# A decoder layer on one core: one joined ones product in each attention

## The chip, the core and the metric

The kernel runs on one core of a Trainium2 chip. Its time is the device time of one execution in microseconds (us); the figure given is the median of several executions. The engines of the core have these names in the profile: PE is TensorE's matmul unit and PEld its weight load, DVE is VectorE, ACT is ScalarE, POOL is GpSimd, and SP is the engine whose queue issues most DMA transfers. Each engine works through its own queue in order; semaphores tie the queues together.

## The reference, cut to what matters

Four inputs of 512 rows and 512 features pass through one decoder layer: a causal self-attention with 16 heads of 32, a causal cross-attention whose keys and values are both the context, and a feed-forward part. All data are float32. The part that the change touches is the softmax of both attentions:

```python
scores = jnp.einsum('bhqd,bhkd->bhqk', q, k) * SCALE
scores = jnp.where(causal, scores, -jnp.inf)
probs = jax.nn.softmax(scores, axis=-1)
ctx = jnp.einsum('bhqk,bhkd->bhqd', probs, v)
```

The cross-attention masks with -10000 in place of minus infinity, so that rows whose visible scores are all very low give weight to masked keys as well. The kernel computes these "masked weights" apart and adds them to numerator and denominator.

## The kernel before

**Layout.** The exponentials are held transposed: keys on the 128 partitions, queries along the free axis. The 16 heads are handled in 4 groups `g` of 4 heads, the 512 keys in 4 blocks `j` of 128. Block `j` of the keys is seen only by the queries from `j*128` on, so a block has 512, 384, 256 or 128 columns. `pts` are two tiles for a unit, each with two of the four heads.

**Units.** An attention (`attend`, L923) walks through ten units, written out by hand at L926 to L929. In this text they are called u0 to u9: (group, block) = (0,0); (0,3)(0,1); (0,2)(1,2); (1,0); (1,3)(1,1); (2,0); (2,3)(2,1); (2,2)(3,2); (3,0); (3,3)(3,1). For each unit `scores` (L385) lets TensorE multiply keys and queries and add the row maxima (L397, L408), ScalarE take the exponential (L431) and POOL zero the masked half of the diagonal blocks (L439). Two units later `values` (L451) lets TensorE use the exponentials. The loop issues the scores of unit n and then the values of unit n-2; the last two units' values come after the loop. All four compute engines run in exactly the order in which the code issues (`BY_HAND`), so what stands earlier in this text stands earlier in the queue.

**Numerator and denominator.** In `shares` (L458) a PSUM pair `pv` of a group has the numerator in half 0 (`u = 0`, exponentials times values) and, for some groups, the denominator in half 1 (`u = 1`, exponentials times a matrix of ones), both at L470. For the groups in `self.added` the denominator is made otherwise: VectorE adds the blocks' exponentials into one tile `sum` (`add_up`, L518), and a single ones product over it (`summed`, L524) gives the denominator. `self.added` is groups 0, 1, 2 in the self-attention and 0, 2 in the cross-attention. The other groups (3; and 1, 3) have one ones product for every block.

**What follows a denominator.** In the self-attention `inverse` (L545 to L548) transposes it, takes the reciprocal and transposes back, on VectorE; POOL scales group 0 to 2 (L540) and VectorE multiplies the last group (L509). The denominator of group 2 is made in a PSUM pair `ls` in unit u8 (L495 to L497). In the cross-attention `divide` (L558, L559) adds the masked weights first. After the self-attention the output projection (L695) follows on TensorE in four quarters, with transposes of the context and of the next input between them (`tp_c`, `tp_a`, L251).

**Masked weights.** `masked` (L373 on ScalarE) and `weigh` (L379 to L381) prepare them. In `attend` VectorE's `weigh` is called at n = 4, 6 or 9 if one is waiting (L956). In three of the four inputs group 2's is made at n = 3; for input 3 at n = 5, with the transposes `mt_c_both` (L353).

**Memory.** PSUM has four pairs in rotation (`ps`): two for a unit's scores, the rest for `pv`, `ls`, `mb` and the transposes. `pt` has six buffers. Tag `xin` has two buffers of 512 columns, into which SP loads the next input for its layer norm (L576).

Of the kernel before, what the change touches and what calls it, by code (L numbers as in the profile page):

```python
# [9 lines left out]
F32 = mybir.dt.float32  # L10
BF16 = mybir.dt.bfloat16
AF = mybir.ActivationFunctionType
ALU = mybir.AluOpType
# [5 lines left out]
P = 128  # L19
# [7 lines left out]
def decoder_layer(  # L27
# [21 lines left out]
    nc = tc.nc  # L49
    B, S, D = x.shape  # L50
    NH = 16
    HD = D // NH
    NT = S // P
    NC = D // P
    HG = P // HD
# [5 lines left out]
    work = ctx.enter_context(tc.tile_pool(name="work", bufs=2))  # L61
# [3 lines left out]
    def pair(name):  # L65

        return ps.tile([P, 2, S], F32, tag="ps", name=name)
# [61 lines left out]
    ones = const.tile([P, HD], F32, name="ones")  # L129
# [8 lines left out]
    zero = const.tile([P, 1], F32, name="zero")  # L138
# [123 lines left out]
    class Attention:  # L262
        def __init__(self, q_t, k_t, v, cross, name):
# [2 lines left out]
            self.more, self.sums, self.rden, self.e = {}, {}, {}, None  # L266
            self.added = (0, 2) if cross else range(NC - 1)

        def maxima(self, pieces):

            at, N = [], 0
            for g, i in pieces:
                at.append(N)
                N += (i + 1) * P
                if g not in self.nm:
                    self.nm[g] = small.tile(
                        [P, NT, HG], F32, tag="nm", name=f"nm_{self.name}_{g}"
                    )  # L280
            name = f"{self.name}_{pieces[0][0]}_{pieces[0][1]}"
            scs = [pair(f"sm_{name}_{n}") for n in range(2)]
            for (g, i), c in zip(pieces, at):
                for r in range(HG):
                    h = slice(r * HD, (r + 1) * HD)
                    nc.tensor.matmul(  # L286
                        scs[r // 2][:, r % 2, c : c + (i + 1) * P],
                        lhsT=self.q_t[h, g, i * P : (i + 1) * P],
                        rhs=self.k_t[h, g, : (i + 1) * P],
                        start=(c == 0),  # L290
                        stop=True,
                        skip_group_check=(c > 0),
                    )
            made = []
            for n in range(2):
                s = work.tile([P, 2, S], F32, tag="pt", name=f"s_{name}_{n}", bufs=6)
                nc.scalar.copy(s, scs[n])  # L297

                if len(pieces) == 1:
                    diagonal = s[:, :, S - P :].unsqueeze(2)  # L300
                elif pieces[0][1] == pieces[1][1]:
                    diagonal = s.rearrange("p u (k q) -> p u k q", k=2)[:, :, :, P:]
                else:
                    diagonal = s[:, :, S - 2 * P :].rearrange("p u (k q) -> p u k q", k=2)
                nc.gpsimd.affine_select(  # L305
                    out=diagonal,
                    in_=diagonal,
                    compare_op=ALU.is_ge,
                    fill=NEG,
                    base=0,  # L310
                    pattern=[[0, 2], [0, len(pieces)], [-1, P]],
                    channel_multiplier=1,
                )
                made.append(s)

            def largest(n, g, i, c):
                nc.vector.tensor_reduce(  # L317
                    self.nm[g][:, i, 2 * n : 2 * n + 2],
                    made[n][:, :, c : c + (i + 1) * P],
                    axis=AX.X,  # L320
                    op=ALU.max,
                    negate=True,
                )

            jobs = [
                (lambda n=n, g=g, i=i, c=c: largest(n, g, i, c))
                for n in range(2)
                for (g, i), c in zip(pieces, at)
            ]
            if pieces == [(pieces[0][0], NT - 1)]:  # L330
                jobs.append(lambda: self.split(pieces[0][0]))
            return jobs
# [125 lines left out]
        def shares(self, g, blocks):  # L458

            js = {j for j, *_ in blocks}  # L460
            first = js == {0} if g % 2 == 0 else js == {2}
            last = js == {2} if g % 2 == 0 else 1 in js
            if first:
                self.pv[g] = pair(f"pv_{self.name}_{g}")
            pv = self.pv[g]
            for u in range(1 if g in self.added else 2):
                for n, (j, c, pts) in enumerate(blocks):
                    for r in range(HG):
                        h = g * HG + r
                        nc.tensor.matmul(  # L470
                            pv[r * HD : (r + 1) * HD, u, j * P :],
                            lhsT=ones if u else self.v[:, j, h * HD : (h + 1) * HD],
                            rhs=pts[r // 2][:, r % 2, c : c + S - j * P],
                            start=first,
                            stop=last and n == len(blocks) - 1,
                            skip_group_check=True,
                        )
            if self.cross:


                if (first if g == 1 else js == {0}) and g - 1 in self.added:
                    self.summed(g - 1, self.pv[g - 1])
                    self.divide(g - 1)
                elif js == {0} and g > 0:
                    self.scale(g - 1)
                if 1 in js and g == NC - 1:
                    self.scale(g - 1)
                if last and g not in self.added:
                    self.divide(g)
                    if g == NC - 1:  # L490
                        self.scale(g)
                return
            if first and g == 0:
                self.out = act.tile([P, NC, S], F32, tag="o_t", name=f"oT_{self.name}")
            if (first if g in self.added else js == {0}) and g - 1 in self.added:  # L495
                self.sum_in = pv if g in self.added else pair(f"ls_{self.name}")
                self.summed(g - 1, self.sum_in)  # L497
            if js == {0} and g - 2 in self.added:
                self.scale(g - 2)
            if 1 in js and g - 1 in self.added and g not in self.added:  # L500
                self.spread(g - 1, self.sum_in)
                self.scale(g - 1)
            if last and g in self.added:
                nc.scalar.copy(self.out[:, g, :], pv[:, 0, :])
                if g > 0:
                    self.spread(g - 1, pv)
            elif last:
                num, den = pv[:, 0, :], pv[:, 1, :]
                nc.vector.tensor_tensor(  # L509
                    self.out[:, g, :], num, self.inverse(g, den), ALU.mult  # L510
                )

        def add_up(self, made):
            for g, j, c, pts in made:
# [408 lines left out]
    def attend(a, late):  # L923


        units = []  # L926
        for g in range(0, NC, 2):
            units += [[(g, 0)], [(g, 3), (g, 1)], [(g, 2), (g + 1, 2)]]
            units += [[(g + 1, 0)], [(g + 1, 3), (g + 1, 1)]]  # L929
        waiting, held, todo = [], [], []  # L930

        def values():
            made = waiting.pop(0)
            a.values(made)

            if len(made) > 1 and made[0][1] == 2:
                held.append(made[1:])
            elif waiting and waiting[0][0][1] > 0:
                if made[0][1] == 0 and held:
                    a.add_up(held.pop())  # L940
                a.add_up(waiting[0] if waiting[0][0][1] == 3 else waiting[0][:1])

        for n, pieces in enumerate(units):
            waiting.append(a.scores(pieces))
            if n in late:
                two = a.cross and late[n] == NC - 1
                both = pair(f"mt_{a.name}_both") if two else None
                copies = a.rows(late[n], both)

                more = [a.masked_sums(2, both)] if two else []  # L950
                for copy in copies:
                    copy(nc.scalar.copy)
                todo.extend(a.masked(*each) for each in more)
            if a.cross and n == 7:
                todo.append(a.masked(*a.masked_sums(3)))
            if n in (4, 6, 9) and todo:  # L956
                todo.pop(0)()
            if n in (3, 4) and put_off:
                put_off.pop(0)()
            if len(waiting) > 2:  # L960
                values()
        while waiting:
            values()

    with tc.manual_schedule(engines=BY_HAND):
# [11 lines left out]
        for b in range(B):  # L977
# [5 lines left out]
            late = with_maxima(between_self, sa, skip, norms)  # L983
# [13 lines left out]
            late = with_maxima(steps[3:], ca)  # L997
# [79 lines left out]
```

## Time and profile before

| what | us |
|---|---|
| median of 3 runs (806.68 to 806.87) | 806.86 |
| the profiled run's own time | 806.75 |
| its span, first to last instruction | 805.0 |
| DVE L518, adding exponentials, self-attention, 72 adds | 59.8 |
| POOL L439, masks of the exponentials, cross / self, 64 / 56 | 53.5 / 48.1 |
| PE L470, ones products of the cross-attention, 64 records each of 512, 384, 256, 128 columns | 8.3, 6.6, 4.9, 3.2 |
| PE L470, ones products of the self-attention, 32 records each of the same | 4.2, 3.3, 2.5, 1.6 |

A float32 product leaves two records, so 64 records of one shape are 32 products: 4 heads, 2 groups, 4 inputs. The four products of a group go to different quarters of the array's columns and run side by side, so the duration of one (592 ns for 512 columns) is much longer than its share of the time. A row of the timeline has the start and the duration in us, then the engine, the line, the operation, the tile written and the tiles read, the shape and how many; in brackets stands how long the engine was idle just before, and what it waited for. Neighbouring instructions of one kind are merged into one row.

### The profile page before, as it was taken

What the parts mean: (1) busy time and instruction counts of PE and PEld (TensorE: products, weight loads), DVE (VectorE), ACT (ScalarE), POOL (GpSimd) and SP (SyncE); (2) the same over time, 40 slices, a digit from 0 to 9 for tenths busy, and PEclk for the clock granted to TensorE, in tenths of its full rate; (3) what the DMA queues carried; (4) which work ended last, traced back from release to release, by engine and by line L of the source; (5) the groups of instructions that cost most, each with busy time, mean ns of one, the idle gap of its engine ahead of it and who ended that gap; (6) DMA issues with size and microseconds to landing.
All of it is one profiled execution on the core that took longest, in us unless ns stands there. A gap on an engine that the chain in (4) does not pass through costs nothing.

```text
span 805.0 us, 13960 instructions
## 1 busy us (share of the span) xinstructions
PE 796.0 (99%) x5612; PEld 380.4 (47%) x5616; DVE 561.4 (70%) x957; ACT 395.6 (49%) x448; POOL 335.8 (42%) x523
## 2 busy tenths in 40 slices
PE   8999999999999999999999999999999999999998
PEld 7444454444444454444544455444444444444544
DVE  2478855879679854587867786587959766988512
ACT  2457516871446615567055742687156833674110
POOL 4334612564234732256333482256423652475100
PEclk9999999999999999999999999999999999999999
DMA  9600000001000000021100000000102000000101
GB/s 336 239 28 28 1 1 1 2 2 53 1 27 27 2 1 0 2 74 33 53 14 14 1 2 1 0 1 2 54 26 80 2 2 0 1 2 2 52 1 52
DMA packets 13681, 24.51 MB, mean 30 GB/s; under 512 B 1968, under 2 KB 2224, under 8 KB 13616
## 3 DMA queue, kind: packets, MB, share of 16 engines
q1 hardware_dynamic: 13184, 22.96, 8.4%
q8 instruction: 44, 0.72, 0.4%
q10 hardware_dynamic: 432, 0.66, 0.2%
q14 instruction: 21, 0.17, 0.1%
HBM read 19.42 MB, written 4.19 MB: 29 GB/s over the span
## 4 chain that ended last, share of the span: by engine, by line
PE 92%; ACT 3%; DVE 3%; issue 1%; DMA 0%
PE pm_qk L235 13%; PE pm_d L223 7%; PE pm_u L235 7%; PE pm_o L695 7%; PE pv_c L470 7%; PE pm_e L223 7%; PE pm_v L223 6%; PE sm_c L286 6%; PE pv_s L470 5%; PE sm_s L286 5%; PE sc_c L397 5%; PE sc_s L397 4%; PE sc_s L408 1%; ACT sum_s L431 1%; DVE nm_s L317 1%; PE sc_c L408 1%
## 5 line engine op out<-in xcount | busy, mean ns | idle before, releaser
L317 DVE TENSOR_REDUCE nm_s<-s_s 128x2 f32<-128x1024 f32 (+3 forms) x128 | 96.9, 810 | 35.2 <-POOL s_s L305 35.2
L317 DVE TENSOR_REDUCE nm_c<-s_c 128x2 f32<-128x1024 f32 (+3 forms) x128 | 95.8, 810 | 31.0 <-POOL s_c L305 31.0
L297 ACT COPY s_s<-sm_s 128x1024 f32<-128x1024 f32 x80 | 77.1, 1015 | 70.7 <-PE sm_s L286 36.4
L297 ACT COPY s_c<-sm_c 128x1024 f32<-128x1024 f32 x80 | 77.1, 1016 | 35.9 <-PE sm_c L286 16.2
L305 POOL TENSOR_SCALAR_AFFINE_SELECT s_c<-s_c 128x512 f32<-128x512 f32 (+1 forms) x80 | 43.9, 550 | 100.4 <-ACT s_c L297 100.4
L305 POOL TENSOR_SCALAR_AFFINE_SELECT s_s<-s_s 128x512 f32<-128x512 f32 (+1 forms) x80 | 43.9, 551 | 96.9 <-ACT s_s L297 96.9
L518 DVE TENSOR_TENSOR sum_s<-sum_s,pt_s 128x256 f32<-128x256 f32 (+2 forms) x72 | 59.8, 896 | 16.7 <-PE pv_s L470 16.7
L431 ACT ACTIVATE pt_c<-sc_c 128x1024 f32<-128x1024 f32 x64 | 61.7, 1031 | 17.7 <-PE sc_c L408 13.8
L439 POOL TENSOR_SCALAR_AFFINE_SELECT pt_c<-pt_c 128x512 f32<-128x512 f32 (+1 forms) x64 | 53.5, 845 | 22.4 <-ACT pt_c L431 22.1
L223 PE MATMUL pm_d<-wdown_sb,hT 128*128 128x512 f32 x128 | 61.5, 610 | 0.0
L431 ACT ACTIVATE pt_s<-sc_s 128x1024 f32<-128x1024 f32 x56 | 53.9, 1029 | 12.6 <-PE sc_s L408 7.0
L235 PE MATMUL pm_u<-fT,wup_sb 128*128 128x512 f32 x128 | 59.3, 604 | 0.0
L223 PE MATMUL pm_v<-wv_sb,xnT 128*128 128x512 f32 x128 | 58.8, 600 | 0.0
L695 PE MATMUL pm_o<-wo_sb,oT_s 128*128 128x512 f32 x128 | 57.8, 596 | 0.0
L235 PE MATMUL pm_qk<-xnT,wk_sb 128*128 128x512 f32 x120 | 57.3, 607 | 0.0
L397 PE MATMUL sc_c<-cqT,ckT 32*128 32x384 f32 (+3 forms) x512 | 56.0, 464 | 0.9 <-ACT sum_c L431 0.9
L235 PE MATMUL pm_qk<-xnT,wq_sb 128*128 128x512 f32 x120 | 56.7, 604 | 0.0
L223 PE MATMUL pm_e<-wexp_sb,fT 128*128 128x512 f32 x120 | 56.3, 604 | 0.0
L397 PE MATMUL sc_s<-qT,kT 32*128 32x128 f32 (+3 forms) x512 | 54.4, 462 | 1.2 <-ACT sum_s L431 0.9
L439 POOL TENSOR_SCALAR_AFFINE_SELECT pt_s<-pt_s 128x512 f32<-128x512 f32 (+1 forms) x56 | 48.1, 868 | 17.6 <-ACT pt_s L431 17.0
L286 PE MATMUL sm_c<-ckT,cqT 32*128 32x512 f32 (+3 forms) x512 | 47.5, 460 | 0.0
L286 PE MATMUL sm_s<-kT,qT 32*128 32x512 f32 (+3 forms) x512 | 47.0, 461 | 0.0
(167 smaller groups left out, 1267.7 us busy)
## 6 DMA issues: line engine op xcount, KB each, us to landing
cv<-in_ctx_dram SPq DMA_DIRECT2D x16, 256.0 KB, 3.6
out_dram<-x SPq DMA_DIRECT2D x15, 256.0 KB, 2.1
x<-in_x_dram SPq DMA_DIRECT2D x14, 256.0 KB, 4.0
xin<-in_x_dram SPq DMA_DIRECT2D x12, 256.0 KB, 2.7
wq_sb<-in_wq_dram SPq DMA_DIRECT2D x2, 512.0 KB, 6.3
wk_sb<-in_wk_dram SPq DMA_DIRECT2D x2, 512.0 KB, 7.9
wv_sb<-in_wv_dram SPq DMA_DIRECT2D x1, 1024.0 KB, 8.3
wo_sb<-in_wo_dram SPq DMA_DIRECT2D x1, 1024.0 KB, 10.1
```

What stands on the lines that cost most here:

```text
L223: nc.tensor.matmul(pm, lhsT=lhs_t[:, c, t * P : (t + 1) * P], rhs=w[:, c, :], start=(c == 0), stop=(c == NC - 1),)
L235: nc.tensor.matmul(pm, lhsT=w[:, c, f * P : (f + 1) * P], rhs=rhs_t[:, c, :], start=(c == 0), stop=(c == NC - 1),)
L286: nc.tensor.matmul(scs[r // 2][:, r % 2, c : c + (i + 1) * P], lhsT=self.q_t[h, g, i * P : (i + 1) * P], rhs=self.k_t[h, g, : (i + 1) * P] ...
L297: nc.scalar.copy(s, scs[n])
L305: nc.gpsimd.affine_select(out=diagonal, in_=diagonal, compare_op=ALU.is_ge, fill=NEG, base=0, pattern=[[0, 2], [0, len(pieces)], [-1, P]], ...
L317: nc.vector.tensor_reduce(self.nm[g][:, i, 2 * n : 2 * n + 2], made[n][:, :, c : c + (i + 1) * P], axis=AX.X, op=ALU.max, negate=True,)
L397: nc.tensor.matmul(scs[r // 2][:, r % 2, c : c + S - j * P], lhsT=self.k_t[h, g, j * P : (j + 1) * P], rhs=self.q_t[h, g, j * P :], start= ...
L431: nc.scalar.activation(pt, scs[n], AF.Exp)
L439: nc.gpsimd.affine_select(out=diagonal, in_=diagonal, compare_op=ALU.is_ge, fill=0.0, base=0, pattern=[[0, 2], [0, len(pieces)], [1, P]], ...
L470: nc.tensor.matmul(pv[r * HD : (r + 1) * HD, u, j * P :], lhsT=ones if u else self.v[:, j, h * HD : (h + 1) * HD], rhs=pts[r // 2][:, r % ...
L518: nc.vector.tensor_tensor(to, to, pts[n][:, :, c : c + S - j * P], ALU.add)
L695: nc.tensor.matmul(pms[t // 2][:, t % 2, :], lhsT=a.out[:, c, t * P : (t + 1) * P], rhs=wo_sb[:, c, :], start=(c == 0), stop=(c == NC - 1),)
```

## The change

In each attention one group that has a ones product for every block is picked, `self.joined`: group 1 in the cross-attention and group 3 in the self-attention. Its block 2 (256 columns, queries 256 to 511) gets no ones product of its own. VectorE adds the exponentials of block 2 to the second half of those of block 0 (`join`) into two new tiles `jn` of tag `xin`, and `joint_sums` makes the ones product of block 0 in two halves: the first half of block 0 itself, and the joined tiles. So four ones products of 256 columns go, and four of 512 become eight of 256.

The joining adds are issued in `values`, when the next unit is the one that begins with block 2 of the group before: after the values of u1 in the cross-attention, of u6 in the self-attention, behind the adds of `add_up` that stand there already.

In the cross-attention the joint product stands where block 0's ones product stood, in u3. In the self-attention (`late`) it is put to the very end: u7 and u8 issue no ones products for group 3, and neither does u8 issue `ls`; after the value products of u9 come `ls`, the ones products of blocks 3 and 1, and the joint product. And `weigh` is called at n = 6 and 9 only, so that group 2's masked weights, where they are ready at n = 3, come two units later.

```diff
+            self.joined, self.joint, self.zero = 1 if cross else NC - 1, [], None
...
             pv = self.pv[g]
+            late = not self.cross and g == self.joined
             for u in range(1 if g in self.added else 2):
+                if u and g == self.joined and 0 in js:
+                    self.zero = blocks[0][2]
+                if u and g == self.joined and (0 in js and not late or 2 in js):
+                    if 0 in js:
+                        self.joint_sums(pv, True)
+                    continue
+                if u and late and 0 in js:
+                    continue
+                if u and late:
+                    self.sum_in = pair(f"ls_{self.name}")
+                    self.summed(g - 1, self.sum_in)
                 for n, (j, c, pts) in enumerate(blocks):
                     for r in range(HG):
...
-                            start=first,
+                            start=first or bool(u and late and n == 0),
                             stop=last and n == len(blocks) - 1,
                             skip_group_check=True,
                         )
+                if u and late:
+                    self.joint_sums(pv, False)
...
-            if (first if g in self.added else js == {0}) and g - 1 in self.added:
-                self.sum_in = pv if g in self.added else pair(f"ls_{self.name}")
-                self.summed(g - 1, self.sum_in)
+            if first and g in self.added and g > 0:
+                self.summed(g - 1, pv)
...
+        def join(self, two, zero):
+
+            (g, _, c, pts), pts0 = two, zero[3]
+            for n in range(2):
+                to = work.tile([P, 2, S // 2], F32, tag="xin", name=f"jn_{self.name}_{n}")
+                nc.vector.tensor_tensor(
+                    to, pts0[n][:, :, S // 2 :], pts[n][:, :, c : c + S // 2], ALU.add
+                )
+                self.joint.append(to)
+
+        def joint_sums(self, pv, start):
+            for n in range(2):
+                for r in range(HG):
+                    nc.tensor.matmul(
+                        pv[r * HD : (r + 1) * HD, 1, n * S // 2 : (n + 1) * S // 2],
+                        lhsT=ones,
+                        rhs=(self.joint if n else self.zero)[r // 2][:, r % 2, : S // 2],
+                        start=start and n == 0,
+                        stop=not start,
+                        skip_group_check=True,
+                    )
...
                 a.add_up(waiting[0] if waiting[0][0][1] == 3 else waiting[0][:1])
+                if waiting[0][0][1] == 2 and waiting[0][1][0] == a.joined:
+                    a.join(waiting[0][1], waiting[1][0])
...
-            if n in (4, 6, 9) and todo:
+            if n in (6, 9) and todo:
                 todo.pop(0)()
```

## The prediction

> **What bounds the kernel.** I read the busy shares, then the chain that ended last, then TensorE's own waits.
>
> ```profile
> PE 796.0 (99%) x5612; PEld 380.4 (47%) x5616; DVE 561.4 (70%) x957; ACT 395.6 (49%) x448; POOL 335.8 (42%) x523
> ...
> PE 92%; ACT 3%; DVE 3%; issue 1%; DMA 0%
> ```
>
> TensorE is busy for 796 of 805 us and carries 92% of the chain; its granted clock is 1.00 throughout. So an edit is worth what it does to TensorE's queue. But a busy figure hides short waits: a product that waits for its second half shows as a long one. In the attention stages I therefore read start times, not sums.
>
> [...]The end of the self-attention of input 1, TensorE first (each product leaves two records, so x8 is four products), then POOL's masks of u8 and u9:
>
> ```profile
> 275.44 0.61 PE L470 MATMUL pv_s<-pt_s,ones 128*32 128x256 f32 x8
> 275.87 1.04 PE L470 MATMUL pv_s<-pt_s,v 128*32 128x512 f32 x8
> 276.73 1.04 PE L470 MATMUL pv_s<-pt_s,ones 128*32 128x512 f32 x8
> 277.59 1.04 PE L524 MATMUL ls_s<-sum_s,ones 128*32 128x512 f32 x8
> 278.44 1.05 PE L470 MATMUL pv_s<-pt_s,v 128*32 128x128 f32 x16
> 279.31 1.05 PE L470 MATMUL pv_s<-pt_s,ones 128*32 128x128 f32 x16
> 280.29 3.70 PE L695 MATMUL pm_o<-wo_sb,oT_s 128*128 128x512 f32 x8
> ...
> 274.31 1.12 POOL L439 TENSOR_SCALAR_AFFINE_SELECT pt_s<-pt_s 128x256 f32<-128x256 f32 x1
> 275.65 0.82 POOL L439 TENSOR_SCALAR_AFFINE_SELECT pt_s<-pt_s 128x512 f32<-128x512 f32 x1 [0.22 <-ACT pt_s L431]
> 276.57 0.95 POOL L439 TENSOR_SCALAR_AFFINE_SELECT pt_s<-pt_s 128x512 f32<-128x512 f32 x1
> ```
>
> See two things. Start to start, four products of 256 columns take 0.43 us and four of 512 take 0.86. And the second mask of u9 ends at 276.57+0.95 = 277.52, while u9's value products start at 278.44: they have 0.92 us of cover, made of the 512-column ones product (0.86) and `ls` (0.86) standing before them.
>
> **1. Products removed.** Each attention loses four ones products of 256 columns (the joined group's block 2): 0.43 us. The four of 512 (block 0) become eight of 256. The Trainium skill, TensorEngine Tiling (Array Packing), Instruction Overhead, speaks against that: some 60 cycles for each matmul. As an estimate, at the 2.4 GHz of its main page (Trainium Kernel Development and Optimization, NeuronCore Architecture) 25 ns for each of the eight added records, 0.2 us an attention, 1.6 in all, if nothing overlaps. The rows say 2 x 0.43 = 0.86, the same as one set of 512. I take the rows: 0; the 1.6 belongs to the high end. At most, then, 8 x 0.43 = 3.4 us is to be had.
>
> **2. Self-attention: the order of the last products.** After: values u7, values u8, values u9, `ls`, ones of u9, joint product. Values of u8 start at 275.44 and need the second u8 mask (274.31+1.12 = 275.43) and a release of 0.05 us (visible below: an add ending at 719.84 releases a weight load at 719.89). They end at 275.48+0.86 = 276.34. Now u9's values are next, 2.1 us earlier than before, and their second half (heads 2 and 3) may start only at 277.52+0.05 = 277.57. Queued behind this wait are `ls`, both ones products and the whole output projection. The mask can't come sooner: it waits for the exponential of u9 and for VectorE's adds, all issued before the first product that the change touches. From 277.57: values and ones of u9 with the change of shape 280.29-278.44 = 1.85, `ls` 0.86, joint product 0.86, so the output projection starts at 281.14 instead of 280.29: **+0.85 us**. The other inputs have the same cover (0.93 to 0.94 us), so 4 x 0.85 = +3.4. Ends: if the mask ran in 0.64 (its time with VectorE silent), 0.31 less; if the split products cost the rule's 0.2, that much more.
>
> Other VectorE and POOL work here. Two joining adds (128x512, 0.55 to 0.95 each) follow the adds that end at 277.02; done by 278.9 at the latest, needed by the joint product at about 280.6. They push the reciprocals of groups 1 to 3 and with them the last multiply (L509), which ends at 282.97, by 1.6 to 1.9, to 284.9 at most. The output projection needs group 3 only in its last quarter, about 295; but the PSUM pair that the multiply frees is taken by the next input's transposes after the first quarter, at 281.14 + 3.53 (280.29 to 283.82) + 0.87 (to 284.69) = 285.5. Cover 0.6 us; without it the wait is what L509 is late. POOL's bias additions move 1.5 us into an idle stretch (10.9 us before its next wait). Cost 0.
>
> **3. Cross-attention, inputs 0 to 2.**
>
> ```profile
> 365.21 1.94 ACT L431 ACTIVATE pt_c<-sc_c 128x1024 f32<-128x1024 f32 x2 [0.29 <-POOL pt_c L439]
> 366.08 0.61 PE L470 MATMUL pv_c<-pt_c,ones 128*32 128x256 f32 x8
> 366.51 1.04 PE L524 MATMUL pv_c<-sum_c,ones 128*32 128x512 f32 x8
> 367.49 1.14 PE L397 MATMUL sc_c<-cqT,ckT 32*128 32x512 f32 x8
> ```
>
> The first product goes; the scores of u5 could start at 367.49-0.43 = 367.06, but the second half needs the PSUM pair that ScalarE leaves at 365.21+1.94 = 367.15, released 367.20. Gain 0.43-0.14 = 0.29. After it the exponentials start from these scores, so the gain stays. VectorE: the joining adds take the slot of the masked weights of group 2 (L379 to L381, 365.42 to 366.95), which move behind group 0's division, into the 3.36 us in which it waited for u4. They need 1.5 to 2 us there: 1.3 left. The joint product reads the sums at about 369.8; the adds are done by 365.47 + 2 x 0.95 = 367.4. 3 x -0.29 = -0.9; ends -0.43 and 0 each.
>
> **4. Cross-attention, input 3.** Another order: masked weights were already late, so nothing moves away to make room.
>
> ```profile
> 717.58 1.71 POOL L833 TENSOR_TENSOR x<-x,some_d 128x512 f32<-128x512 f32 x1
> 719.24 1.09 POOL L439 TENSOR_SCALAR_AFFINE_SELECT pt_c<-pt_c 128x512 f32<-128x512 f32 x1
> 719.36 1.59 PE L524 MATMUL pv_c<-sum_c,ones 128*32 128x512 f32 x8
> 719.89 0.14 PEld L524 LDWEIGHTS pv_c<-sum_c,ones 128*32 128x32 f32 x4 [0.42 <-DVE sum_c L518]
> 721.60 0.68 DVE L559 TENSOR_TENSOR behT<-pv_c,behT 128x512 f32<-128x512 f32 x1
> 722.33 0.23 PEld L353 LDWEIGHTS <-parts 128*128 128x128 bf16 x4 [0.81 <-DVE behT L559]
> ```
>
> The sum over group 0 is waited for already: TensorE, 0.43 us earlier, still resumes at 719.89. Gain 0. Then the transposes at 722.33 wait for the PSUM pair that L559 frees, and the two joining adds now stand before L558 and L559. By the row of these adds (128x512 in the cross-attention, mean 954 ns) L559 would end near 722.9: +0.6. The Trainium skill, SBUF — State Buffer, Who interferes with whom: a VectorE operation with two SBUF inputs and a GpSimd operation that reads SBUF lock each other out, the later one for all of the other. The trace agrees: the add issued at 718.07 took 1.77 us and ended 0.55 after POOL's L833 (719.29). By turns, then: mask to 720.33, add to 720.88, mask to 721.37, add to 721.92 with POOL's next L833 held back; L558 and L559 (one PSUM input, not held in this trace beside L833) to 723.13; transposes at 723.19 instead of 722.34: **+0.85**. I take the lock; ends 0 and +1.3.
>
> **5. DMA.** The joined tiles share two buffers with the next input's `xin` loads, which now wait for the joint product (about 171 and 371) and, for input 3, stand behind the output store and the load of x (345.6 to 361.5). First read at 212.07 and 409.49, landing 2.7 us: 35 us of cover. Cost 0.
>
> **Sum.** +3.4 -0.9 +0.85 = +3.4 on the profiled run's 806.75 (span 805.0), hence 806.86+3.4 = 810.2 for the median; I say **810.2**.
>
> **Rivals.**
> - *The saving arrives*: masks in time, 4 x 0.43 + 0.9 = 2.6 us, 804.3; with the whole 3.4, 803.4. For: 99% busy. Against: 277.52 stands against 276.34. Chance 0.06.
> - *It cancels*: self stalls of 0.3, input 3 free: 4 x 0.3 - 0.9 = +0.3, 807.2. For: overlap of the two halves. Against: a queue that waited as a whole at 719.36. 0.07.
> - *The joining adds decide* on VectorE's tail: a PSUM pair late by 1 us at the transposes between the output projection's quarters, three times, beside the forecast: 813.2. For: VectorE is busy without a gap from 265.16 to 282.97. Against: the 0.6 us of cover. Decides once the last multiply ends after 285.5. 0.07.
>
> Forecast 0.80, its own range 808.8 to 811.7; the whole range, 808.4 to 811.8, takes in four faster masks (-1.2) with part of the cross ends (-0.6), and above the split's 1.6. The medians lie within 0.02%, so 0.2% (1.6 us) is about what can be told from no change. Slower holds forecast and adds, 0.87; same 0.07; faster 0.06.
>
> **What would show it.** Step 2: TensorE (or its weight loads) waiting about 1.2 us for POOL's `pt_s` in each self-attention, and the output projection 5.7 us after the first value product of u8, where it was 280.29-275.87 = 4.42. Step 3: the second half of u5's scores 1.12 us after group 0's ones product starts, 0.98 before. Step 4: the transposes 3.3 us after the release at 719.89 by the lock, 3.0 by the mean, 2.44 before. If the output projection follows u8's values in about 4.0 us, the first step is wrong and with it the sign.

## The result, and the profile after

The changed kernel takes 810.23 us (median of 6 runs, 810.15 to 810.63) against 806.82 us for the kernel before (6 runs, 806.68 to 806.87): 1.0045 times as long, 95% interval 1.0034 to 1.0055. The forecast was 810.2.

First the page of the changed kernel: the busy time of each engine, and the shares of the chain that ended last.

```profile
PE 797.0 (99%) x5616; PEld 384.9 (48%) x5616; DVE 573.0 (71%) x973; ACT 395.5 (49%) x448; POOL 337.5 (42%) x523
...
PE 86%; DVE 6%; ACT 4%; POOL 2%; issue 1%; DMA 0%; ACTq 0%; DVEq 0%
```

Products were removed, and still TensorE's busy time is not lower: 797.0 us after 796.0. The chain tells more: TensorE's share has gone from 92% to 86%, and POOL, which did not appear in it, has 2%. The end is now set in places by other engines.

The end of the self-attention of input 1 in the timeline of the changed kernel: TensorE's rows, then POOL's two masks of u9 in one row, then VectorE's joining adds and its last multiply.

```profile
275.37 2.38 PE L484 MATMUL pv_s<-pt_s,v 128*32 128x256 f32 x28
278.38 1.06 PE L484 MATMUL pv_s<-pt_s,v 128*32 128x128 f32 x12 [0.63 <-POOL pt_s L441]
279.06 1.23 PE L561 MATMUL ls_s<-sum_s,ones 128*32 128x512 f32 x8
279.92 1.24 PE L484 MATMUL pv_s<-pt_s,ones 128*32 128x128 f32 x16
280.78 0.81 PE L541 MATMUL pv_s<-pt_s,ones 128*32 128x256 f32 x8
281.21 0.81 PE L541 MATMUL pv_s<-jn_s,ones 128*32 128x256 f32 x8
281.95 3.70 PE L732 MATMUL pm_o<-wo_sb,oT_s 128*128 128x512 f32 x8
...
276.47 1.85 POOL L441 TENSOR_SCALAR_AFFINE_SELECT pt_s<-pt_s 128x512 f32<-128x512 f32 x2 [0.23 <-ACT pt_s L433]
...
277.75 1.72 DVE L533 TENSOR_TENSOR jn_s<-pt_s,pt_s 128x512 f32<-128x512 f32 x2
...
284.43 0.69 DVE L524 TENSOR_TENSOR oT_s<-pv_s,dt_s 128x512 f32<-128x512 f32 x1
```

POOL's second mask ends at 276.47+1.85 = 278.32, and the second half of u9's value products starts at 278.38, with POOL as its releaser. Every TensorE row below it in the list stood behind it in the queue. The first value product of u8 is inside the merged first row; the single records have it at 276.26. From there to the output projection it is 281.95-276.26 = 5.69 us, where it was 4.42. The 0.63 us in brackets is only a part of the wait: heads 0 and 1 had waited for the first mask before that, inside the first row. The value products of u8 were through at about 276.26+0.86 = 277.12, so from there to the second half of u9 it is 1.26 us.

The middle of the cross-attention of input 1: the product of the sum over group 0, the scores of u5, the value products of u3; then the value products of u3 in the kernel before.

```profile
367.75 1.04 PE L561 MATMUL pv_c<-sum_c,ones 128*32 128x512 f32 x8
368.72 1.27 PE L399 MATMUL sc_c<-cqT,ckT 32*128 32x512 f32 x8
369.68 0.53 PE L410 MATMUL sc_c<-mrow_c,onesb 32*128 32x512 bf16 x4
370.14 1.06 PE L484 MATMUL pv_c<-pt_c,cv 128*32 128x512 f32 x8
...
368.77 1.06 PE L470 MATMUL pv_c<-pt_c,cv 128*32 128x512 f32 x8
```

The row of the scores is 1.27 us long where it was 1.14: a short wait inside a product row, as in the first section of the prediction. The values come 370.14-367.75 = 2.39 us after the sum's product, 368.77-366.51 = 2.26 before. So 0.13 of the 0.43 us is lost again.

The cross-attention of input 3: POOL's put-off additions and masks, VectorE's joining adds and the two additions of the division, TensorE's weight loads.

```profile
720.63 1.70 POOL L870 TENSOR_TENSOR x<-x,some_d 128x512 f32<-128x512 f32 x1
722.29 2.12 POOL L441 TENSOR_SCALAR_AFFINE_SELECT pt_c<-pt_c 128x512 f32<-128x512 f32 x2
...
722.81 2.15 DVE L533 TENSOR_TENSOR jn_c<-pt_c,pt_c 128x512 f32<-128x512 f32 x2
724.88 0.68 DVE L595 TENSOR_TENSOR ct_c<-pv_c,ct_c 128x512 f32<-128x512 f32 x1
...
722.94 0.14 PEld L561 LDWEIGHTS pv_c<-sum_c,ones 128*32 128x32 f32 x4 [0.84 <-DVE sum_c L555]
...
726.21 0.23 PEld L355 LDWEIGHTS <-parts 128*128 128x128 bf16 x4 [1.64 <-DVE behT L596]
```

The wait for the sum has grown from 0.42 to 0.84 us: TensorE came 0.43 us earlier and found the sum no earlier. Then the transposes stand 726.21-722.94 = 3.27 us after that release, 2.44 before.

Both traces, laid over each other by the starts of TensorE's rows, give the whole difference by place:

| place | predicted us | measured us |
|---|---|---|
| start of the work (first transposes) | 0 | +0.27 |
| self-attention, inputs 0, 1, 2, 3 | +0.85 each | +0.85, +0.85, +1.15, +0.85 |
| cross-attention, inputs 0, 1, 2 | -0.29 each | -0.30, -0.30, -0.31 |
| cross-attention, input 3 | +0.85 | -0.43 at the sum's arrival, +0.43 and +0.83 after it: +0.83 |

That is +3.89 for a span that went from 805.0 to 808.9. The profiled execution was the longest of its six (810.63); the spans of the others are 808.4 to 808.8. The +0.27 at the start is no part of the change: from run to run the first transposes of all kernels here begin between 8.11 and 8.61 us.

### The profile page after: what moved, and what is told of

Same layout as the page of the kernel before. It is cut to its first block, busy times and chain, and to the rows that moved or that the text cites. A ratio compares the mean times of both kernels' runs of the same rounds, so it can differ in the third digit from the quotient of the medians.

```text
span 808.9 us, 13968 instructions
## 1 busy us (share of the span) xinstructions
PE 797.0 (99%) x5616; PEld 384.9 (48%) x5616; DVE 573.0 (71%) x973; ACT 395.5 (49%) x448; POOL 337.5 (42%) x523
## 4 chain that ended last, share of the span: by engine, by line
PE 86%; DVE 6%; ACT 4%; POOL 2%; issue 1%; DMA 0%; ACTq 0%; DVEq 0%
PE pm_qk L235 13%; PE pm_u L235 7%; PE pm_o L732 7%; PE pm_e L223 7%; PE pm_d L223 6%; PE pm_v L223 6%; PE pv_c L484 6%; PE sm_s L288 5%; PE sm_c L288 5%; PE sc_c L399 4%; PE sc_s L399 3%; PE pv_s L484 3%; POOL pt_s L441 2%; DVE nm_c L319 2%; ACT sum_s L433 1%
```

## The experiments

Ten kernels. The kernel before was run beside each batch; its median there is given with the result.

### The self-attention alone

```diff
-            self.joined, self.joint, self.zero = 1 if cross else NC - 1, [], None
+            self.joined, self.joint, self.zero = None if cross else NC - 1, [], None
...
-            if n in (6, 9) and todo:
+            if n in (4, 6, 9) and todo:
```

> The change in the self-attention alone; cross-attention and masked weights as before. Theory of the prediction (u9's value products wait for POOL's second mask, 0.85 us in each of four inputs): +3.4 on 806.8, so 810.2, and the output projection starts 5.7 us after the first value product of u8. Rival, the loss of the changed kernel is made in the cross-attention: at or below 806.8 (down to 805.1 with 0.43 saved four times).

810.46 us against 806.65 (ratio 1.0049, 1.0036 to 1.0061). By place: +0.85, +0.85, +1.14, +0.85. The loss of the whole change is made in the self-attention.

### The cross-attention alone

```diff
-            self.joined, self.joint, self.zero = 1 if cross else NC - 1, [], None
+            self.joined, self.joint, self.zero = 1 if cross else None, [], None
```

The place of `summed(g - 1)` in the self-attention goes back to that of the kernel before.

> The change in the cross-attention alone, with the masked weights two units later; self-attention as before. Theory of the prediction: three inputs gain 0.3 each, input 3 loses 0.85, so -0.05: 806.75, not to be told from 806.8; the transposes of input 3 come 3.3 us after the release of the sum of group 0, 2.44 before. Rival, the loss is made here: 810. Rival, the saving arrives in all four: 805.1 to 805.9.

806.93 us against 806.65 (0.9995 to 1.0012). By place: -0.30, -0.30, -0.30, +0.83; the transposes of input 3 stand 3.27 us after the release. Gain and loss cancel, as expected.

### The whole change without the self-attention's joining adds

```diff
-                    a.join(waiting[0][1], waiting[1][0])
+                    if a.cross:
+                        a.join(waiting[0][1], waiting[1][0])
```

> The whole change without the self-attention's two joining adds: the second half of the joint product reads the second half of block 0 itself, so that block 2 is left out of group 3's denominators there. Theory (the order costs): between 809.0 (the second mask of u9 freed from VectorE's adds, 0.3 less in each input) and 810.2. Rival, the joining adds make the loss: 806.8 or less.

810.40 us against 806.65 (1.0035 to 1.0060). The wait at u9's value products is 0.62 us with POOL as releaser, as it was with the adds (0.63), and the places read +0.85, +0.85, +1.14, +0.85. So the joining adds cost nothing in the self-attention, neither by themselves nor through the masks, and the allowance of 0.31 us for a freed mask was not needed. The order of the products costs.

### The self-attention in another order

```diff
                 if u and late and 0 in js:
+                    self.joint_sums(pv, True, (0,))
+                    self.sum_in = pair(f"ls_{self.name}")
+                    self.summed(g - 1, self.sum_in)
                     continue
-                if u and late:
-                    self.sum_in = pair(f"ls_{self.name}")
-                    self.summed(g - 1, self.sum_in)
...
-                    self.joint_sums(pv, False)
+                    self.joint_sums(pv, False, (1,))
```

The rest is the self-attention alone; the new last argument of `joint_sums` says which of the two halves it makes.

> As the self-attention alone, but u8 issues the first half of the joint product and the product of the sum over group 2 before u9's value products; u9 issues only the half with the joined tiles. Theory (the order, not the joining, costs): 0.43 + 0.86 us now stand before u9's values and the mask needs 1.23, so the wait goes and 0.43 is saved in each input: 806.8 - 1.7 = 805.1, with the output projection about 4.0 us after the first value product of u8. If the mask is late by 0.3 in some inputs, 805.5. Rival, the joining adds on VectorE decide: 806.8 or slower, with the transposes between the quarters of the output projection late by what the last multiply is late.

806.45 us against 806.65 (0.9989 to 1.0007). The order takes the loss away, 4.0 us against the self-attention alone. But the saving did not come: by the trace 0.08 an input in place of 0.43. The output projection stands 280.24-275.47 = 4.77 us after the first value product of u8. The 4.0 of the expectation had counted the removed 0.43 us twice, since u8's values start 0.43 earlier as well: without a wait it would be about 4.43, and 0.34 is what is lost. The timeline of this kernel, same place: TensorE's product of the sum over group 2, its weight loads, VectorE's last add of that sum.

```profile
276.76 1.39 PE L561 MATMUL ls_s<-sum_s,ones 128*32 128x512 f32 x8
...
277.10 0.14 PEld L561 LDWEIGHTS ls_s<-sum_s,ones 128*32 128x32 f32 x4 [0.22 <-DVE sum_s L555]
...
277.60 0.61 PEld L484 LDWEIGHTS pv_s<-pt_s,v 128*32 128x32 f32 x12 [0.29 <-POOL pt_s L441]
...
275.93 1.11 DVE L555 TENSOR_TENSOR sum_s<-sum_s,pt_s 128x512 f32<-128x512 f32 x1
```

The row of `ls` is 1.39 us long in place of 1.04: its second half (heads 2 and 3) waits for VectorE's last add, which ends at 275.93+1.11 = 277.04. In the single records heads 0 and 1 of `ls` start at 276.76, heads 2 and 3 at 277.10. This lag stays between the two halves until the last product (0.37 us there), and the output projection waits for the later half. This expectation had counted the mask and forgotten the sum: the 0.86 us of the old ones product covered both.

### The same order with other work as cover

The first product of the output projection (group 0, rows 0 to 127) is issued between the first half of the joint product and `ls`.

```diff
                     self.joint_sums(pv, True, (0,))
+                    self.fill()
...
+    def first_product(e, a):
+        e.pm = pair(f"pm_o{e.b}_0")
+        nc.tensor.matmul(
+            e.pm[:, 0, :], lhsT=a.out[:, 0, :P], rhs=wo_sb[:, 0, :],
+            start=True, stop=False,
+        )
```

> As the run with the self-attention's other order, with the first of the sixteen products of the output projection (group 0, first 128 rows, 0.86 us) issued between the first half of the joint product and the product of the sum over group 2. Theory (the ones product that was taken away had covered VectorE's last add of that sum, whose second tile comes 0.34 us late in the other order): the wait for the sum goes, and the output projection's second product starts about 0.4 us earlier than before in each input, less up to 0.25 for two more changes between products of 32 and of 128 columns: 0.2 to 0.43 in each, so 805.0 to 805.9. Rival (the end is set elsewhere, on VectorE's chain of reciprocals): 806.5 as without the filling, with the transposes between the quarters late.

806.90 us against 806.79 (0.9992 to 1.0009): no gain, where 0.9 to 1.8 us was expected. TensorE's rows of this kernel:

```profile
276.28 0.67 PE L542 MATMUL pv_s<-pt_s,ones 128*32 128x256 f32 x8
276.89 1.12 PE L730 MATMUL pm_o<-wo_sb,oT_s 128*128 128x512 f32 x2
277.94 1.06 PE L562 MATMUL ls_s<-sum_s,ones 128*32 128x512 f32 x8
278.82 1.05 PE L485 MATMUL pv_s<-pt_s,v 128*32 128x128 f32 x16
```

No row has a wait left, and the rows are within 0.06 us of their old lengths. But from the ones product to the output projection's product it is 0.61 us, 0.18 more than the 0.43 of its work, and from there to `ls` 1.05, 0.19 more than 0.86. Two changes between products of 32 and of 128 columns cost 0.37 of the 0.43 us; the expectation had allowed 0.25 for them. The rival (VectorE's chain) fails: the transposes between the quarters follow each other as before.

### The split alone

Block 0's ones product of the two groups in two halves, in the kernel before; nothing joined.

```diff
+                    for n in range(2):
+                        half = slice(n * S // 2, (n + 1) * S // 2)
...
+                                rhs=blocks[0][2][r // 2][:, r % 2, half],
```

> The kernel before with one thing changed: block 0's ones product of group 1 (cross-attention) and of group 3 (self-attention) is made in two halves of 256 columns, eight products in place of four, at the same place; nothing is joined or removed. By the rows of the trace (eight of 256 take as long as four of 512): 806.7, no change. By a fixed price for each matmul of 25 ns, eight more records in each of eight attentions: +1.6, 808.3.

806.83 us against 806.79 (0.9992 to 1.0009). Laid over the kernel before, no TensorE row moves by more than 0.08 us against the start of the work. The rows were right; a fixed price of 25 ns for each added record does not show at 256 columns.

### Input 3: the joining adds behind the division's additions

```diff
             nc.vector.tensor_tensor(beh, pv[:, 0, :], beh, ALU.add)
+            if g == 0 and self.hold:
+                self.hold()
```

`hold` is the call of `join` in input 3; the rest is the cross-attention alone.

> As the cross-attention alone, but input 3 issues its two joining adds behind the two additions of group 0's division. Theory (the transposes of input 3 wait because the joining adds stand ahead of these additions): the transposes come 2.44 us after the release of the sum of group 0, as before, and 0.83 us comes back: 0.8 less than with the cross-attention alone, 806.1. Rival (GpSimd's additions or the wait for the sum itself make the loss): no change against the cross-attention alone, 806.9.

806.13 us against 806.79 (0.9983 to 1.0001). The transposes come 2.44 us after the release of the sum, as before the change, and the time is 0.8 less than with the cross-attention alone (806.93, run in another batch; by the two traces 0.79). So what costs is that the adds stand ahead of the division. Placed there, they take 1.28 us for the two, not 2.15.

### Input 3: GpSimd's put-off additions two units later

One line, alone in the kernel before; then with the cross-attention joined, in its own order and with the adds held as above.

```diff
-            if n in (3, 4) and put_off:
+            if n in (5, 6) and put_off:
```

> The kernel before, with GpSimd's two put-off additions of the last cross-attention issued two units later (units 5 and 6 in place of 3 and 4). Theory (VectorE's adds and these additions lock each other out ahead of the sum of group 0): the third of VectorE's adds takes about 0.7 us in place of 1.77, TensorE's wait of 0.42 us for the sum goes, and the wait of the transposes shrinks: -0.4 to -0.8, so 805.9 to 806.3. Rival (no lock): 806.7.

> The change in the cross-attention alone, in its own order, with GpSimd's two put-off additions two units later. Theory (in input 3 the joining adds cost only because the additions on GpSimd stretch them and the sum before them): the two joining adds take 1.4 us and fit into the 1.7 us in which VectorE waited for the product of the sum, TensorE waits neither there nor longer at the transposes, and input 3 gains the 0.43 of the removed products on top of the 0.5 of the moved additions: 806.8 - 0.9 - 0.5 - 0.4 = 805.0; with the score tiles late as in the other inputs 805.2. Rival (the joining adds cost at the transposes wherever GpSimd's additions stand): 806 or slower.

> As the run with the put-off additions two units later and the cross-attention joined, but input 3's joining adds behind the two additions of group 0's division. Theory (with the additions away the joining adds have room ahead of the division): the same time within 0.2. Rival (they have no room): up to 0.8 less.

Alone: 806.59 us against 806.79 (0.9988 to 1.0006), not told apart by the medians, and short of the 805.9 to 806.3 expected. In the trace the theory is right: the last add of the sum takes 0.68 us in place of 1.77, TensorE's wait of 0.42 us for the sum is gone, and the scores of u5 start 0.52 us earlier. But the end of the span takes 0.36 us of that back (last section). Joined: 805.79 us against 806.66 (0.9980 to 0.9997), slower than the 805.0 to 805.2 expected. With the adds held: **805.32 us against 806.66 (ratio 0.9984, 0.9975 to 0.9993)**, below both kernels of this study. Of the joined kernel in its own order, VectorE's rows and the transposes:

```profile
717.62 1.72 DVE L534 TENSOR_TENSOR jn_c<-pt_c,pt_c 128x512 f32<-128x512 f32 x2
719.26 0.68 DVE L596 TENSOR_TENSOR ct_c<-pv_c,ct_c 128x512 f32<-128x512 f32 x1
...
720.59 0.40 PE L355 MATMUL mt_c_both<-identb,parts 128*128 128x128 bf16 x4 [0.26 <-DVE behT L597]
```

And with the adds held:

```profile
719.01 0.69 DVE L597 TENSOR_TENSOR ct_c<-pv_c,ct_c 128x512 f32<-128x512 f32 x1 [1.28 <-PE pv_c L563]
719.62 0.68 DVE L598 TENSOR_TENSOR behT<-pv_c,behT 128x512 f32<-128x512 f32 x1
720.21 1.28 DVE L535 TENSOR_TENSOR jn_c<-pt_c,pt_c 128x512 f32<-128x512 f32 x2
...
720.35 0.40 PE L356 MATMUL mt_c_both<-identb,parts 128*128 128x128 bf16 x4
```

There are three lengths for the same two adds, and the single records show why: an add that is issued while one of GpSimd's masks runs ends 0.54 us after that mask. In the changed kernel both adds meet a mask (they end at 723.92 and 724.96, the masks at 723.38 and 724.42): 2.15 us. In the joined kernel only the second does (719.34, the mask 718.79): 1.72. With the adds held neither does: 1.28. So the put-off additions don't stretch the joining adds themselves; they had held up the sum before them. VectorE's gap was 1.28 us, not the 1.7 that I had taken from the run with the additions moved alone, because TensorE's sum product now comes 0.43 us earlier too. So 1.72 in the gap leaves a wait of 0.26 us at the transposes: "fits" was wrong, and of the cost that the rival saw wherever the additions stand, 0.26 of 0.83 us is left. The medians differ by 0.47, the traces by 0.24.

## Why the prediction was right

**Products removed.** The 0.43 us an attention and the price of nothing for the split both held; the split alone shows the second.

**Self-attention.** The step held as it was put: the second mask, not the joining, sets when the queue goes on, and everything behind waits. The whole change without the adds has the same loss; the other order is without it. VectorE's tail was covered as said: the last multiply ended at 285.12, before its PSUM pair was wanted.

Wrong was one term: "the other inputs have the same cover". In input 2 the loss was 1.15, and the traces of all three kernels with this order have it (1.15, 1.14, 1.14). It begins ahead of the first product that the change touches, in work that the prediction took as unchanged. ScalarE's exponential of u7 starts at 467.94 after 0.30 us of idle time; in the kernel before, and in the kernels with the other order, it follows the work ahead of it at once. By the times of the trace the delay passes on to POOL's next mask, to VectorE's adds (0.3 to 0.5 us later against TensorE than before) and to the exponentials of u9 (0.14 and 0.31), and the second mask ends 0.3 us later. Why the exponential of u7 is late, and in this input alone, stays open.

One of its signs was set wrong too. For masks in time it named about 4.0 us from u8's first value product to the output projection; by its own rows it is 4.43, since both move by 0.43. The measured 5.69 is clear of both.

**Cross-attention, inputs 0 to 2.** -0.29 was said, -0.30 measured, with the predicted wait at ScalarE's PSUM pair (0.13 us for 0.14), and the moved masked weights cost nothing. Neither did the shared `xin` buffers: the table by place leaves no loss for them.

**Input 3.** Between the lock (+0.85) and the mean of the row (+0.6) the lock decided: +0.83, and the adds, additions and transposes come at the predicted times plus the 3.05 us by which this place had moved. Each joining add ended 0.54 us after the mask that it met, where the forecast's turns had 0.55. The Trainium skill is borne out here (SBUF — State Buffer, Who interferes with whom): adds with two SBUF inputs are held up by GpSimd's reading operations beside them.

**The sum.** The medians differ by 3.41, and +3.4 was said. That it fits so closely is in part luck: without the start the places sum to 3.62, because input 2's extra 0.3 was not foreseen, and the runs' starts alone differ by up to 0.5. Of the rivals, "the saving arrives" and "it cancels" fall with the 5.69 us, "the joining adds decide" with the run without them.

## What to carry to other kernels

A product on the busiest engine can be cover: before removing or moving it, list every input of the work queued behind it with the time it arrives (here a mask and a sum on two engines), and only what is left after the latest of them is saved. An add moved to another engine is priced at the place where it lands, by what stands behind it and by what runs beside it, not by its row's mean. Filling a gap with foreign work costs too, if the array has to change its shape (here 0.37 of the 0.43 us to be had).

## What the runs showed of the hardware

- A change between products of 32 and of 128 columns cost 0.18 and 0.19 us around the filling product. Where the kernel before makes it, from u9's ones products to the output projection, it cost 280.29-279.31-0.86 = 0.12 us. The Trainium skill (TensorEngine Tiling (Array Packing), Key Properties) says that changing the tiling mode drains the engine; no run here shows the draining itself, only these prices.
- Four products that run side by side in the array's quarters did not level out: with the self-attention's other order two of them start 0.34 us late at `ls` (277.10 after 276.76); five sets of products later, at the joint product, the lag is 0.37 us, and the later half decides.
- In the three kernels with the put-off additions moved, the last product started 0.7 to 2.0 us earlier than before, but the span ended 4.08 us after that start instead of 3.72. The last store was issued earlier by the full amount, and the span ended 0.36 us later after it than before; why was not tried.
